# The sending tables of the last five node blocks are made first, the receiving tables behind everything, in a graph-network kernel

## The chip, the cores and the metric

The kernel runs on one core of a Trainium2 chip. The core has five engines with an instruction queue each: TensorE (PE, with its weight loads counted apart as PEld), VectorE (DVE), ScalarE (ACT), GpSimd (POOL) and SyncE (SP). SyncE and ScalarE issue ordinary transfers, GpSimd issues gathers; all are carried by the core's 16 DMA engines. The metric is the device time of the program in microseconds (us); lower is better.

## What is computed

A graph has N = 3125 nodes with 128 features, and 100000 edges, sorted by their destination. Each edge has 16 attributes and one of R = 4 types. Two layers follow each other; shortened:

```python
# layer 0
summed = segment_sum(x[src], dst)
x = layernorm(x + elu(summed / max(deg, 1) @ W + b))
# layer 1, with h = x, four heads of 128 columns, HC = 512
xl = einsum('nf,rfh->nrh', h, W_l) + b_l
xr = einsum('nf,rfh->nrh', h, W_r) + b_r
z = leaky_relu(xl[src, edge_type] + xr[dst, edge_type] + e_feat, 0.2)
score = einsum('ehc,ehc->eh', z, att[edge_type])
alpha = softmax of score over the edges with one dst and one edge_type
agg = segment_sum(xl[src, edge_type] * alpha, dst * R + edge_type)
h1 = layernorm(h + gate-weighted mean over types and heads of agg)
x = layernorm(x + layernorm(h1 + ffn(h1)))
```

`xl` is called the sending table here: row (node, type) is what a node gives to its outgoing edges. `xr` is the receiving table: what a node adds to its incoming edges.

## The kernel before

**Tiling.** Edges are cut into 784 tiles of 128; four tiles are a unit u, so there are 196 units. Nodes are cut into 25 blocks of 128 (`NB2` = 25). Edges are sorted by destination, so a tile receives at a few neighbouring nodes, but its sources lie anywhere.

**Layer 0, up to about 1080 us.** For each tile GpSimd gathers x[src] (64 KB), TensorE sums the rows by destination and VectorE adds the result to `acc0`. When the edges of a block are through, `block(b, s)` (line 1263) finishes the block in small steps: `take`, `mean` and `stats` (normalization), `turn` (transpose to `ht`), `tables` and `half`. They are put into a table of steps with `at_step`, and the loop over s (lines 1362 to 1402) issues each step's pieces on the engines in an order written out by hand; blocks 20 to 24 have steps pressed closer together. The class `Ordered` (line 629) fixes this order on each engine, and since it issues the instructions, most of them carry its line, 647, in the profile.

**Tables.** For each type r, `tables` has TensorE make a receiving tile `xq` and a sending tile `xp`, 128x512 each, in PSUM: one matmul with the bias (`two`, `cbl`), then h times `wr` or `wl`. Three PSUM buffers `xp` serve both. ScalarE copies the sending tile and four more columns to `xlr` (line 647, three buffers). `half(r)`, one step later, has SyncE write `xlr` to the DRAM table `xl_d` (258 KB), VectorE split the receiving tile into a rounded high part and the remainder (`xh`, three buffers; a copy and a subtraction), and SyncE write both parts to the DRAM table `xr_d` (512 KB). There are 100 of each over the run. Each block also writes its `ht` to `ht_d`.

**Between the layers.** ScalarE's queue loads all of `ht_d` into `acc1` (1600 KB). Constants are made, and flags are computed that say whether the edges suit this tiling (`bad`, 15 columns, lines 1476 to 1534); if not, the function `general` runs afterwards. Three of the ten buffers `xl` serve these flags as scratch.

**Attention, to about 2750 us.** The loop over s (from -2) does parts of several units per step. SyncE loads the codes of a unit (`sg`, `lb`, `load_codes`), its attributes `ers` and masks `rm`, and the windows `win` of the receiving table (`load_rows`, 15 buffers, lines 1561 to 1578). GpSimd gathers four tiles of `xl_d` per unit, 258 KB each, into `xl` (`load`, ten buffers, so up to ten units ahead, of which three wait for the flags' scratch). `z_of` sums one head's edge features, the window picked by a one-hot (`oht`) and the transposed `xl` on TensorE into `z`; ScalarE makes `relu`, TensorE the `row` of scores, VectorE the softmax, and TensorE the weighted sums `ag`, which VectorE adds to `acc1`. The only order across engines is that of data and of buffers. Buffers of all these lie in one pool, `at` (line 1408), whose memory layer 0 used before; DRAM tables are tracked as a whole, so a read of `xr_d` or `xl_d` waits for every write to it that was issued before.

**After attention.** The feed-forward part and two normalizations, some 60 us.

Of the kernel before, what the change touches and what calls it, by code (L numbers as in the profile page):

```python
# [20 lines left out]
P = 128  # L21
N = 3125
E = 100000
F = 128
R = 4
H = 4
HC = H * F
# [17 lines left out]
F32R = mybir.dt.float32r  # L45
# [573 lines left out]
WW = 16  # L619
# [9 lines left out]
NP = 3200  # L629
NB2 = NP // P  # L630
NPW = NP + WQ
XW = HC + H
RW = 4 * P + 2
# [30 lines left out]


UD, ND, SHI = 72, 240, NB2
SEG = ((0, 52), (52, UD))


# [23 lines left out]
def windows(ctx: ExitStack, tc: tile.TileContext, a, out, flag):  # L693
    nc = tc.nc
    cst = ctx.enter_context(tc.tile_pool(name="cst", bufs=1))
    dram = ctx.enter_context(tc.tile_pool(name="fdram", bufs=1, space=DRAM))
# [6 lines left out]
    lb_d = dram.tile([NQ // 4, P, 16 * H * R], F32, name="lb_d")  # L703
    v2_d = dram.tile([P, H], F32, name="v2_d")
    xl_d = dram.tile([NP * R, XW], F32, name="xl_d")
    xr_d = dram.tile([NP * R * 2, HC], F32, name="xr_d")
    h_d = dram.tile([NB2, P, F], F32, name="fh_d")
    ht_d = dram.tile([P, NP], F32, name="ht_d")
    ident = cst.tile([P, P], F32, name="f_ident")
# [4 lines left out]
    tb = S["tb"] = cst.tile([16, 2 * TT + 1], BF16, name="tb")  # L714
    tk = S["tk"] = cst.tile([16, 2 * TT], BF16, name="tk")
    ns2 = S["ns2"] = cst.tile([16, 2 * TT], BF16, name="ns2")
    bad = cst.tile([P, 15], F32, name="bad")
    iw = cst.tile([P, P], F32, name="iw")
    pid = cst.tile([P, 1], I32, name="pid")
    ir = cst.tile([P, R], F32, name="ir")  # L720
# [12 lines left out]
    def of_tile(t, col):  # L733
        return bass.IndirectOffsetOnAxis(ap=col[:, t:t + 1], axis=0)

    xr_n = xr_d.rearrange("(n k) c -> n k c", k=2 * R)

    def node(t, eng):
        return nc.values_load(d0_i[0:1, t:t + 1], engines=[eng], min_val=0, max_val=N - 1,
# [17 lines left out]
    with tc.tile_pool(name="l0c", bufs=1) as l0c:  # L757
# [14 lines left out]
        with tc.tile_pool(name="pr", bufs=1) as pr, tc.tile_pool(name="prp", bufs=2, space=PSUM) as prp:  # L772
# [94 lines left out]
            rm = pr.tile([TR, TC, RW], BF16, name="rm")  # L867
            b, k, f, l = (rm[:, :, o:o + P] for o in (0, P + 2, 2 * P + 2, 3 * P + 2))
# [14 lines left out]

        with tc.tile_pool(name="m0c", bufs=1) as m0c, tc.tile_pool(name="l0", bufs=2) as l0, \
                tc.tile_pool(name="l0e", bufs=1) as l0e, tc.tile_pool(name="m0", bufs=2) as m0, \
                tc.tile_pool(name="l0p", bufs=1, space=PSUM) as l0p, \
                tc.tile_pool(name="m0p", bufs=1, space=PSUM) as m0p:
            pe, ve, act, sp = (Ordered(tc, e) for e in (nc.tensor, nc.vector, nc.scalar, nc.sync))
# [15 lines left out]
            wr = m0c.tile([F, R, HC], F32, name="wr")  # L904
            fb = wl.rearrange("p r w -> p (r w)")[:, :TT]

            cbl = m0c.tile([P, R, XW], F32R, name="cbl")
            two = m0c.tile([P, 2, P], F32R, name="two")
# [73 lines left out]
            def halves(s, r, p0, row, n):  # L982

                d = {}

                def high():
                    d["hi"] = m0.tile([1, 2, XW], F32R, name="xh", bufs=3)
# [270 lines left out]


            xl_v = xl_d.rearrange("(b p r) w -> b p r w", p=P, r=R)  # L1260
            xr_v = xr_d.rearrange("(b p r s) w -> b p r (s w)", p=P, r=R, s=2)

            def block(b, s):
                n = min(P, N - b * P)
                d = {}

                def new(name, shape, bufs=3, dt=F32):
                    d[name] = m0.tile(shape, dt, name=name, bufs=bufs)
                    return d[name]
# [37 lines left out]
                def turn():  # L1307
                    sp.dma_start(h_d[b], d["y0"])
                    htp = m0p.tile([P, F], F32, name="mw")
                    pe.transpose(htp, d["y0"], ident)  # L1310
                    act.activation(new("ht", [P, F], 2), htp, AF.Copy)

                def tables():
                    xa = m0p.tile([P, R, H], F32, name="mw")
                    pe.matmul(xa, two[:, 0], cbl[:, :, HC:], start=True, stop=False)
                    pe.matmul(xa, d["ht"], wl[:, :, HC:], start=False, stop=True)
                    for r in range(R):
                        xp, xq = (m0p.tile([P, HC], F32, name="xp", bufs=3) for _ in range(2))
                        for o, w, i, c in ((xq, wr[:, r], 1, cbl[:, r, :HC]), (xp, wl[:, r, :HC], 0, cbl[:, r, :HC])):
                            pe.matmul(o, two[:, i], c, start=True, stop=False)  # L1320
                            pe.matmul(o, d["ht"], w, start=False, stop=True)
                        xl = d["xl", r] = m0.tile([P, XW], F32, name="xlr", bufs=3)
                        xh = d["xh", r] = m0.tile([P, 2, HC], F32R, name="xh", bufs=3)
                        act.activation(xl[:, :HC], xp, AF.Copy)
                        act.activation(xl[:, HC:], xa[:, r], AF.Copy)
                        d["xq", r] = xq

                def half(r):
                    if r == 0:
                        sp.dma_start(ht_d[:, b * P:(b + 1) * P], d["ht"])  # L1330
                    xh = d["xh", r]
                    sp.dma_start(xl_v[b][:, r], d["xl", r])
                    ve.tensor_copy(xh[:, 0], d["xq", r])
                    ve.tensor_sub(xh[:, 1], d["xq", r], xh[:, 0].bitcast(F32))
                    sp.dma_start(xr_v[b][:, r], xh.bitcast(F32).rearrange("p s w -> p (s w)"))

                if b >= NB2 - 5:
                    at_step(s - 2, "sp", early)
# [21 lines left out]
            for s in range(last + 1):  # L1360
# [40 lines left out]
                for us in edges:  # L1401
                    keep(us)


    acc1 = ctx.enter_context(tc.tile_pool(name="ac1", bufs=1)).tile([P, NPW], F32, name="acc1")
    nc.gpsimd.memset(acc1[:, NP:], 0.0)
    nc.scalar.dma_start(acc1[:, :NP], ht_d)
    with tc.tile_pool(name="ac", bufs=1) as ac, tc.tile_pool(name="at", bufs=2) as at, \
            tc.tile_pool(name="atp", bufs=1, space=PSUM) as atp:


# [60 lines left out]
        nc.vector.tensor_scalar(acc1[:, :NP], acc1[:, :NP], gbt, None, op0=OP.add)  # L1472


        rf, rl, rs = (at.tile([P, 4, XW], F32, name="xl", bufs=10).rearrange("p a b -> p (a b)") for _ in range(3))
        nc.sync.dma_start(rf[:16, :2 * TT], bass.AP(tensor=fl_d.tensor, offset=fl_d.offset, ap=[[0, 16], [1, 2 * TT]]))
        rF, rL = (rf[:16, i * TT:(i + 1) * TT] for i in range(2))
        rF4, rL4 = (x[0:1].rearrange("p (u i) -> p u i", i=4) for x in (rF, rL))
# [48 lines left out]
        count(7, NQ)  # L1527
        o1 = ac.tile([P, 1], F32, name="o1")
        nc.vector.memset(o1, 1.0)
        bp = atp.tile([1, 15], F32, name="row", bufs=2)  # L1530
# [20 lines left out]

        def load_codes(u):
            d = Q[u] = {}
            d["sg"] = at.tile([P, 512], BF16, name="sg", bufs=4)
            sv = S["seg_d"][u * 4:u * 4 + 4, :]
            sp.dma_start(d["sg"], bass.AP(tensor=sv.tensor, offset=sv.offset, ap=[[0, P], [1, 512]]))
            if u % 4 == 0:
                LB[u // 4] = at.tile([P, 4, 4, H, R], F32, name="lb")
                sp.dma_start(LB[u // 4].rearrange("p j t h r -> p (j t h r)"), lb_d[u // 4])

        def load_rows(u):
            d = Q[u]
            d["er"] = ers[:, u % NE]
            sp.dma_start(d["er"][:2 * DE].bitcast(F32), eat_d[u])
            if u % 2 == 0:
                g = G[u // 2] = {}
                g["rm"] = at.tile([P, RW], BF16, name="rm", bufs=6)
                rv_ = S["rm_d"][u * 4:u * 4 + 8, :]
                sp.dma_start(g["rm"], bass.AP(tensor=rv_.tensor, offset=rv_.offset, ap=[[RW, 8], [0, 16], [1, RW]]))

            d["w"] = []
            for i, k in windows_of(u):
                n = WW if k > 1 else W
                n4 = node(u * 4 + i, ENG.SP)
                w = at.tile([P, HC], F32R, name="win", bufs=15)
                sp.dma_start(w[:n * 2 * R].bitcast(F32), xr_n[ds(n4, n)].rearrange("n k c -> (n k) c"))
                d["w"].append((w, slice(i * P, (i + k) * P), n * 2 * R))

        def load(u):
            d = Q[u]  # L1580
            d["xl"] = at.tile([P, 4, XW], F32, name="xl", bufs=10)
# [402 lines left out]
```

## Time and profile before

| what | value |
|---|---|
| three runs | 2867.88, 2873.77, 2883.67 us |
| median | 2873.77 us |
| profiled execution, as a run | 2875.92 us |
| its span, first to last instruction | 2874.1 us |
| mean granted TensorE clock | 0.898 |
| PE busy | 2417.7 us (84%) |
| DVE busy | 1821.4 us (63%) |
| POOL busy | 1245.1 us (43%) |
| ACT busy | 908.9 us (32%) |
| gathers of `xl_d` | 784, 959 ns each on POOL |
| VectorE's copy to `xh`, 128x512 | 100, 690 ns each |
| ScalarE's copy to `xlr`, 128x512 | 100, 597 ns each |

How to read it: a profile line begins with a time or a line and engine, then an operation with what it writes and reads. "Idle before" is the gap before an instruction on its own engine, with what ended it; "issue" is a gap in which the engine waited for nothing that the profile shows. The rows of digits cut the span into 40 slices of 71.9 us and give the busy tenths of each. The chain of waits goes back from the last instruction, at each step to what released it. A table by stretches gives, for each stretch of time, the busy time of each engine with the number of its instructions, the granted clock, the share of the DMA engines that was busy, and GB/s.

### The profile page before, as it was taken

What the parts mean: (1) busy time and instruction counts of PE and PEld (TensorE: products, weight loads), DVE (VectorE), ACT (ScalarE), POOL (GpSimd) and SP (SyncE); (2) the same over time, 40 slices, a digit from 0 to 9 for tenths busy, and PEclk for the clock granted to TensorE, in tenths of its full rate; (3) what the DMA queues carried; (4) which work ended last, traced back from release to release, by engine and by line L of the source; (5) the groups of instructions that cost most, each with busy time, mean ns of one, the idle gap of its engine ahead of it and who ended that gap; (6) DMA issues with size and microseconds to landing.
All of it is one profiled execution on the core that took longest, in us unless ns stands there. A gap on an engine that the chain in (4) does not pass through costs nothing.

```text
span 2874.1 us, 66163 instructions
## 1 busy us (share of the span) xinstructions
PE 2417.7 (84%) x24485; PEld 1858.4 (65%) x24485; DVE 1821.4 (63%) x6395; ACT 908.9 (32%) x1964; POOL 1245.1 (43%) x1294
## 2 busy tenths in 40 slices
PE   3687777877777685699999999999999999999974
PEld 2454454445444443577777777888888888888853
DVE  6655535653544345377777777777777777776656
ACT  0121112212222231244444444444444443333314
POOL 6555443444434413244444444444444444444400
PEclk9757778878888787799999999999999999999977
DMA  4323344444455456466666667777777789999910
GB/s 128 90 73 104 112 137 142 138 125 155 147 186 173 139 197 227 128 210 205 205 205 208 205 205 216 235 236 235 236 235 233 235 241 245 254 243 246 236 53 24
DMA packets 284394, 520.64 MB, mean 181 GB/s; under 512 B 45833, under 2 KB 144820, under 8 KB 283151
## 3 DMA queue, kind: packets, MB, share of 16 engines
q1 hardware_dynamic: 201588, 273.76, 30.7%
q0 software_dynamic: 78592, 239.71, 29.6%
q8 instruction: 194, 3.18, 0.5%
q10 hardware_dynamic: 3880, 2.84, 0.4%
q14 instruction: 140, 1.15, 0.1%
HBM read 412.10 MB, written 104.82 MB: 180 GB/s over the span
## 4 chain that ended last, share of the span: by engine, by line
PE 48%; DVE 8%; issue 3%; DMA 2%; ACT 0%; SPq 0%; DVEq 0%; ACTq 0%
PE z L647 30%; PE ag L647 7%; PE row L647 6%; DVE wo L647 4%; PE e L647 2%; PE sm_p L647 2%; DMA win<-xr_d 1%; DVE f L647 0%; DVE oh L647 0%; DVE ea L647 0%; PE f L1930 0%; PE f L1922 0%; DVE acc L647 0%; DMA xr_d<-xh 0%; DVE fst L1886 0%
## 5 line engine op out<-in xcount | busy, mean ns | idle before, releaser
L647 POOL DMA_INDIRECT xl<-xl_d,src_e x784 | 751.5, 959 | 895.8 <-PE ag L647 391.5
L647 POOL DMA_INDIRECT xg<-in_x_dram,src_e x496 | 489.0, 986 | 542.6 <-PE sg L647 368.5
L647 ACT ACTIVATE relu<-z 128x512 f32<-128x512 f32 x784 | 449.1, 597 | 793.7 <-PE z L647 611.1
L647 PE MATMUL z<-f_ident,xl 128*128 128x128 f32 x3136 | 476.1, 274 | 0.0
L647 PEld LDWEIGHTS z<-f_ident,xl 128*128 128x128 f32 x3136 | 368.7, 141 | 44.3 <-issue 0.6
L647 PE MATMUL z<-ea,weh 128*128 128x512 f32 x784 | 360.9, 460 | 18.4 <-issue 14.1
L647 PE MATMUL z<-oht,win 96*128 96x128 f32 (+2 forms) x1600 | 343.4, 297 | 4.1 <-DMA win<-xr_d 2.2
L647 PEld LDWEIGHTS z<-oht,win 128*128 128x128 f32 (+1 forms) x1600 | 275.4, 190 | 60.6 <-issue 3.2
L647 PE MATMUL z<-ea,wel 128*128 128x512 f32 x784 | 310.1, 395 | 0.1
L647 PE MATMUL row<-relu,attw 128*32 128x128 f32 x6272 | 247.7, 277 | 31.1 <-issue 29.4
L647 PE MATMUL ag<-xl,wo 128*32 128x128 f32 x6272 | 225.6, 279 | 7.5 <-DVE acc L647 4.2
L647 PEld LDWEIGHTS row<-relu,attw 128*32 128x32 f32 x6272 | 172.6, 109 | 85.0 <-issue 84.0
L647 PE MATMUL xp<-cbl,two 128*128 128x512 f32 x200 | 165.4, 827 | 30.5 <-DVE xh L647 13.1
L647 DVE TENSOR_TENSOR acc<-acc,fo 128x128 f32 x124 | 35.3, 285 | 245.0 <-remote 97.9
L647 PEld LDWEIGHTS ag<-xl,wo 128*32 128x32 f32 x6272 | 181.1, 112 | 9.1 <-DVE acc L647 5.1
L647 DVE TENSOR_TENSOR_SCAN m<-rm,row 128x128 f32<-128x128 bf16 x98 | 41.2, 420 | 228.4 <-PE row L647 228.4
L647 PE MATMUL fo<-ic,il 128*128 128x300 bf16 x744 | 153.5, 357 | 37.4 <-DVE acc L647 31.3
L647 DVE CAST xh<-xp 128x512 fp32r<-128x512 f32 x100 | 69.0, 690 | 157.3 <-PE xp L647 113.7
L647 PEld LDWEIGHTS z<-ea,weh 128*128 128x128 f32 x784 | 149.5, 191 | 27.5 <-issue 27.5
L647 ACT ACTIVATE xlr<-xp 128x512 f32<-128x512 f32 x100 | 59.7, 597 | 304.3 <-PE xp L647 156.2
L647 PEld LDWEIGHTS z<-ea,wel 128*128 128x128 f32 x784 | 150.1, 191 | 9.0 <-issue 0.4
L647 DVE SCALAR_TENSOR_TENSOR ea<-far,e 128x512 fp32r<-128x512 bf16 x196 | 132.2, 675 | 36.7 <-remote 35.6
(327 smaller groups left out, 4059.3 us busy)
## 6 DMA issues: line engine op xcount, KB each, us to landing
win<-xr_d SPq DMA_DIRECT2D x224, 256.0 KB
xr_d<-xh SPq DMA_DIRECT2D x100, 512.0 KB
win<-xr_d SPq DMA_DIRECT2D x176, 192.0 KB
xl_d<-xlr SPq DMA_DIRECT2D x100, 258.0 KB
sg<-seg_d SPq DMA_DIRECT2D x196, 128.0 KB
rm<-rq_d SPq DMA_DIRECT2D x98, 128.5 KB
eat_d<-emt SPq DMA_DIRECT2D x196, 64.0 KB
xl<-xl_d,src_e POOLq DMA_INDIRECT x784
```

Of the source, the lines that this page charges most:

```text
L647: ins = f(*args, **kw)
```

## The change

The last five blocks (`NL` = 5, blocks 20 to 24) make only their sending tables in `tables`. Their receiving tables follow after the whole loop over steps, in a loop of their own over 20 (block, type) pairs; there ScalarE, not VectorE, makes the high part, and ScalarE's queue, not SyncE's, issues the write. The transposed blocks `ht` are kept for this in five buffers.

The receiving table becomes two DRAM tables. Blocks 0 to 19 go to `xr_a`; blocks 19 to 24 go to `xr_b`, so block 19 is written to both. Units below `UL` = 175 take their windows from `xr_a`, the others from `xr_b`. Two more flags check that the edges allow this.

What the receiving tables need (`wr`, `cbl`, `two`, `xh`, `ht`) moves to a pool `m0r` of its own. Attention's buffers are split into three pools: `ax` for `xl`, `ay` for `sg`, `lb`, `rm` and `win`, `at` for the rest; numbers of buffers stay.

```diff
+NL, UL = 5, 175
-    xr_d = dram.tile([NP * R * 2, HC], F32, name="xr_d")
+    xr_a, xr_b = (dram.tile([NP * R * 2, HC], F32, name=n) for n in ("xr_a", "xr_b"))
-    bad = cst.tile([P, 15], F32, name="bad")
+    bad = cst.tile([P, 17], F32, name="bad")
+                tc.tile_pool(name="m0r", bufs=1) as m0r, \
...
+            def table(o, ht, w, i, r):
+                pe.matmul(o, two[:, i], cbl[:, r, :HC], start=True, stop=False)
+                pe.matmul(o, ht, w, start=False, stop=True)
+
+            def receiving(b, r, xq, copy):
+                xh = m0r.tile([P, 2, HC], F32R, name="xh", bufs=3)
+                copy(xh[:, 0], xq)
+                ve.tensor_sub(xh[:, 1], xq, xh[:, 0].bitcast(F32))
+                return [(x[b][:, r], xh.bitcast(F32).rearrange("p s w -> p (s w)"))
+                        for x, y in ((xra_v, b < NB2 - NL), (xrb_v, b >= NB2 - NL - 1)) if y]
...
-                    act.activation(new("ht", [P, F], 2), htp, AF.Copy)
+                    d["ht"] = HT[b] = m0r.tile([P, F], F32, name="ht", bufs=NL)
+                    act.activation(d["ht"], htp, AF.Copy)
...
                     for r in range(R):
-                        xp, xq = (m0p.tile([P, HC], F32, name="xp", bufs=3) for _ in range(2))
-                        for o, w, i, c in ((xq, wr[:, r], 1, cbl[:, r, :HC]), (xp, wl[:, r, :HC], 0, cbl[:, r, :HC])):
-                            pe.matmul(o, two[:, i], c, start=True, stop=False)
-                            pe.matmul(o, d["ht"], w, start=False, stop=True)
+                        if b < NB2 - NL:
+                            xq = d["xq", r] = m0p.tile([P, HC], F32, name="xp", bufs=3)
+                            table(xq, HT[b], wr[:, r], 1, r)
+                        xp = m0p.tile([P, HC], F32, name="xp", bufs=3)
+                        table(xp, HT[b], wl[:, r, :HC], 0, r)
...
                     sp.dma_start(xl_v[b][:, r], d["xl", r])
-                    ve.tensor_copy(xh[:, 0], d["xq", r])
-                    ve.tensor_sub(xh[:, 1], d["xq", r], xh[:, 0].bitcast(F32))
-                    sp.dma_start(xr_v[b][:, r], xh.bitcast(F32).rearrange("p s w -> p (s w)"))
+                    if b < NB2 - NL:
+                        for o, x in receiving(b, r, d["xq", r], ve.tensor_copy):
+                            sp.dma_start(o, x)
...
+            for b in range(NB2 - NL, NB2):
+                for r in range(R):
+                    xq = m0p.tile([P, HC], F32, name="xp", bufs=3)
+                    table(xq, HT[b], wr[:, r], 1, r)
+                    for o, x in receiving(b, r, xq, lambda o, x: act.activation(o, x, AF.Copy)):
+                        act.dma_start(o, x)
...
-    with tc.tile_pool(name="ac", bufs=1) as ac, tc.tile_pool(name="at", bufs=2) as at, \
+    with tc.tile_pool(name="ac", bufs=1) as ac, tc.tile_pool(name="ax", bufs=10) as ax, \
+            tc.tile_pool(name="ay", bufs=2) as ay, tc.tile_pool(name="at", bufs=2) as at, \
             tc.tile_pool(name="atp", bufs=1, space=PSUM) as atp:
...
+        nc.vector.tensor_scalar(bad[0:1, 15:16], rL[0:1, 4 * UL - 1:4 * UL], float(P * (NB2 - NL) - WW), None,
+                                op0=OP.is_gt)
+        nc.vector.tensor_scalar(bad[0:1, 16:17], rF[0:1, 4 * UL:4 * UL + 1], float(P * (NB2 - NL - 1)), None,
+                                op0=OP.is_lt)
...
-                sp.dma_start(w[:n * 2 * R].bitcast(F32), xr_n[ds(n4, n)].rearrange("n k c -> (n k) c"))
+                sp.dma_start(w[:n * 2 * R].bitcast(F32),
+                             (xra_n if u < UL else xrb_n)[ds(n4, n)].rearrange("n k c -> (n k) c"))
```

More of the change, by code (lines that the diff above doesn't have):

```diff
@@ L734, in of_tile @@
         return bass.IndirectOffsetOnAxis(ap=col[:, t:t + 1], axis=0)
-    xr_n = xr_d.rearrange("(n k) c -> n k c", k=2 * R)
+    xra_n, xrb_n = (x.rearrange("(n k) c -> n k c", k=2 * R) for x in (xr_a, xr_b))
     def node(t, eng):
@@ L903, in windows @@
             wl = m0c.tile([F, R, XW], F32, name="wl")
-            wr = m0c.tile([F, R, HC], F32, name="wr")
+            wr = m0r.tile([F, R, HC], F32, name="wr")
             fb = wl.rearrange("p r w -> p (r w)")[:, :TT]
-            cbl = m0c.tile([P, R, XW], F32R, name="cbl")
-            two = m0c.tile([P, 2, P], F32R, name="two")
+            cbl = m0r.tile([P, R, XW], F32R, name="cbl")
+            two = m0r.tile([P, 2, P], F32R, name="two")
             nc.vector.memset(cbl.bitcast(F32), 0.0)
@@ L986, in high @@
                 def high():
-                    d["hi"] = m0.tile([1, 2, XW], F32R, name="xh", bufs=3)
+                    d["hi"] = m0r.tile([1, 2, XW], F32R, name="xh", bufs=3)
                     act.activation(d["hi"][:, 0, :n], row()[:, :n], AF.Copy)
@@ L1260, in windows @@
             xl_v = xl_d.rearrange("(b p r) w -> b p r w", p=P, r=R)
-            xr_v = xr_d.rearrange("(b p r s) w -> b p r (s w)", p=P, r=R, s=2)
+            xra_v, xrb_v = (x.rearrange("(b p r s) w -> b p r (s w)", p=P, r=R, s=2) for x in (xr_a, xr_b))
+            HT = {}
+            def table(o, ht, w, i, r):
[7 more added lines that the diff above has]
+                        for x, y in ((xra_v, b < NB2 - NL), (xrb_v, b >= NB2 - NL - 1)) if y]
             def block(b, s):
@@ L1317, in tables @@
                     for r in range(R):
-                        xp, xq = (m0p.tile([P, HC], F32, name="xp", bufs=3) for _ in range(2))
-                        for o, w, i, c in ((xq, wr[:, r], 1, cbl[:, r, :HC]), (xp, wl[:, r, :HC], 0, cbl[:, r, :HC])):
-                            pe.matmul(o, two[:, i], c, start=True, stop=False)
-                            pe.matmul(o, d["ht"], w, start=False, stop=True)
+                        if b < NB2 - NL:
[3 more added lines that the diff above has]
+                        table(xp, HT[b], wl[:, r, :HC], 0, r)
                         xl = d["xl", r] = m0.tile([P, XW], F32, name="xlr", bufs=3)
-                        xh = d["xh", r] = m0.tile([P, 2, HC], F32R, name="xh", bufs=3)
                         act.activation(xl[:, :HC], xp, AF.Copy)
                         act.activation(xl[:, HC:], xa[:, r], AF.Copy)
-                        d["xq", r] = xq
                 def half(r):
@@ L1330, in half @@
                         sp.dma_start(ht_d[:, b * P:(b + 1) * P], d["ht"])
-                    xh = d["xh", r]
                     sp.dma_start(xl_v[b][:, r], d["xl", r])
-                    ve.tensor_copy(xh[:, 0], d["xq", r])
-                    ve.tensor_sub(xh[:, 1], d["xq", r], xh[:, 0].bitcast(F32))
-                    sp.dma_start(xr_v[b][:, r], xh.bitcast(F32).rearrange("p s w -> p (s w)"))
+                    if b < NB2 - NL:
+                        for o, x in receiving(b, r, d["xq", r], ve.tensor_copy):
+                            sp.dma_start(o, x)
                 if b >= NB2 - 5:
@@ L1472, in windows @@
         nc.vector.tensor_scalar(acc1[:, :NP], acc1[:, :NP], gbt, None, op0=OP.add)
-        rf, rl, rs = (at.tile([P, 4, XW], F32, name="xl", bufs=10).rearrange("p a b -> p (a b)") for _ in range(3))
+        rf, rl, rs = (ax.tile([P, 4, XW], F32, name="xl", bufs=10).rearrange("p a b -> p (a b)") for _ in range(3))
         nc.sync.dma_start(rf[:16, :2 * TT], bass.AP(tensor=fl_d.tensor, offset=fl_d.offset, ap=[[0, 16], [1, 2 * TT]]))
@@ L1529, in windows @@
         nc.vector.memset(o1, 1.0)
-        bp = atp.tile([1, 15], F32, name="row", bufs=2)
+        bp = atp.tile([1, 17], F32, name="row", bufs=2)
         nc.tensor.matmul(bp, o1, bad, start=True, stop=True)
@@ L1553, in load_codes @@
             d = Q[u] = {}
-            d["sg"] = at.tile([P, 512], BF16, name="sg", bufs=4)
+            d["sg"] = ay.tile([P, 512], BF16, name="sg", bufs=4)
             sv = S["seg_d"][u * 4:u * 4 + 4, :]
@@ L1557, in load_codes @@
             if u % 4 == 0:
-                LB[u // 4] = at.tile([P, 4, 4, H, R], F32, name="lb")
+                LB[u // 4] = ay.tile([P, 4, 4, H, R], F32, name="lb")
                 sp.dma_start(LB[u // 4].rearrange("p j t h r -> p (j t h r)"), lb_d[u // 4])
@@ L1566, in load_rows @@
                 g = G[u // 2] = {}
-                g["rm"] = at.tile([P, RW], BF16, name="rm", bufs=6)
+                g["rm"] = ay.tile([P, RW], BF16, name="rm", bufs=6)
                 rv_ = S["rm_d"][u * 4:u * 4 + 8, :]
@@ L1574, in load_rows @@
                 n4 = node(u * 4 + i, ENG.SP)
-                w = at.tile([P, HC], F32R, name="win", bufs=15)
-                sp.dma_start(w[:n * 2 * R].bitcast(F32), xr_n[ds(n4, n)].rearrange("n k c -> (n k) c"))
+                w = ay.tile([P, HC], F32R, name="win", bufs=15)
+                sp.dma_start(w[:n * 2 * R].bitcast(F32),
+                             (xra_n if u < UL else xrb_n)[ds(n4, n)].rearrange("n k c -> (n k) c"))
                 d["w"].append((w, slice(i * P, (i + k) * P), n * 2 * R))
@@ L1580, in load @@
             d = Q[u]
-            d["xl"] = at.tile([P, 4, XW], F32, name="xl", bufs=10)
+            d["xl"] = ax.tile([P, 4, XW], F32, name="xl", bufs=10)
             for i in range(4):
```

## The prediction

> **What bounds the kernel now.** I read the page first: which engine fills which stretch of the span, and which chain ended last.
>
> ```profile
> span 2874.1 us, 66163 instructions
> PE   3687777877777685699999999999999999999974
> DMA  4323344444455456466666667777777789999910
> PE 48%; DVE 8%; issue 3%; DMA 2%; ACT 0%; SPq 0%; DVEq 0%; ACTq 0%
> ```
>
> From about 1190 us on (slice 17 of 40) TensorE is at nine tenths or more: attention is TensorE's, and no line of the change alters what TensorE does there. Before that nothing is full. So the change can only move the moment at which attention reaches its full speed, and every microsecond of that is a microsecond of the whole. Next I took the chain of waits around that moment:
>
> ```profile
> 1104.18 7.41 PE xp L647 x21
> 1111.58 1.52 issue
> 1113.10 0.67 ACT xlr L647 x2
> 1113.79 0.32 SPq L647
> 1114.20 8.05 DMA xr_d<-xh
> 1122.45 0.32 SPq L1476
> ...
> 1128.73 4.08 DMA ers<-eat_d
> 1132.81 0.25 issue
> 1133.06 4.64 PE z L647 x14
> ...
> 1172.92 0.37 PE row L647
> 1173.29 2.42 issue
> ```
>
> The last block's tables end at 1113, the last receiving write lands at 1122.25, and then everything that attention loads is let go at once. The first z (a 128x512 score tile) starts at 1133.06. But TensorE then falls into single instructions with 1 to 2.5 us of "issue" between them. The table by stretches and GpSimd's timeline tell when:
>
> ```profile
> 1115.00:1120.00 5.00, 0.00 (x0) 0.00 (x0) 1.89 (x1) 0.00 (x0) 0.00 (x0) 0.74 0.99 395
> 1130.00:1140.00 10.00, 6.89 (x27) 5.38 (x28) 8.75 (x27) 2.51 (x4) 7.56 (x9) 0.61 1.03 329
> 1160.00:1170.00 10.00, 1.53 (x4) 0.51 (x4) 0.00 (x0) 0.00 (x0) 7.56 (x9) 0.50 0.76 209
> 1180.00:1190.00 10.00, 10.00 (x81) 8.17 (x81) 4.01 (x11) 4.36 (x9) 0.00 (x0) 0.89 0.21 68
> 1123.21 0.95 POOL L647 DMA_INDIRECT xl<-xl_d,src_e  x1 [39.67 <-DVE xl L1493]
> 1173.55 0.95 POOL L647 DMA_INDIRECT xl<-xl_d,src_e  x1 [0.30 <-issue]
> ```
>
> (Columns of the stretches: length, busy PE, weight load, DVE, ACT, POOL, granted clock, DMA share, GB/s.) Forty gathers of the sending table go out back to back, one per 1.254 us, from 1123.21 to 1173.55; from the 16th on PE, DVE and ACT hardly move, and all is full again near 1178, 3.5 us after the last. I call this the stutter. It isn't bytes: the same shows at the start of layer 0, where gathers run unbroken from 50.67 to 76.7 at a DMA share of 0.18 to 0.21 and PE, ACT and DVE stand still until 80. In attention proper, four gathers per 7.9 us do no harm. By 1143 TensorE had done some 9 us of attention, so the kernel before is worth an attention that starts at full speed at 1177.8 - 9 = about **1168.5**. That is my zero.
>
> **What the Trainium skill says.** "Runtime: NRT & Kernel Launch", Instruction fetch mechanics: each engine has a small first-in-first-out memory of instructions, refilled in 16 KiB blocks over a DMA queue of its own. That fits the stutter: the trace has two packets on the q8 instruction queue between 1100 and 1185, at 1102.4 and 1182.1, and none in the stutter. That a stream of gathers keeps the refill out no run here shows; I use it as a guess. "DMA: Bandwidth & Descriptors", Issuing engines are not separate DMA queues: writes from ScalarE's queue run on the same 16 engines as SyncE's and GpSimd's. The trace agrees: 1130 to 1140 has gathers and loads together at a share of 1.03 and 329 GB/s. So moving the receiving writes to ScalarE saves issue time only, not transfer time.
>
> **The change part by part.** All against the profiled execution (span 2874.1 us, 2875.9 us as a run; the median of the three runs is 2873.8, so I subtract from that).
>
> *Send side, sooner.* A table costs TensorE 1.09 us (1069.49, 1070.58, 1071.67 in its timeline). Blocks 20, 21, 22 lose four receiving tables each, 12 x 1.09 = 13 us. After the last layer-0 gather (1033.8) nothing comes from outside, and each burst of eight tables (8.8 us; block 22's runs to 1073.8) stands in TensorE's order ahead of the aggregation that the next block waits for, so I take the whole 13 as path: layer 0's last additions from 1077 to 1064. Blocks 23 and 24 lose 8 x 1.09 = 8.7 us out of 1091.05 to 1113.0. Tables end near 1113 - 13 - 8.7 = 1091; ScalarE's copy and its four columns 0.8, SyncE's issue 0.3, landing of 258 KB on a queue that is no longer full about 2.5 us instead of 8.05: the last sending write lands near 1095, the first gather starts near **1096** instead of 1123.2, and GpSimd's stream ends near 1096 + 50 = 1146. Bounds: 20 us (half of the 13 hidden) to 32 us sooner. The gathers no longer wait for any receiving write.
>
> *Receive side, later.* All 20 tables of blocks 20 to 24 stand in TensorE's order ahead of attention's first e and z, and attention's general pool lies on the memory of xh, so VectorE's first memset of a carry, the one-hots queued behind it and TensorE's first z wait for the landing of the last xr_b write. The start of attention is therefore T = last xr_b landing + 1.5 us. Per table: TensorE 1.09, ScalarE's copy 0.60 (as the 128x512 xlr copy), VectorE's subtraction 0.69, ScalarE's issue about 0.4, a 512 KB write. By engine time alone that is 1.1 us each. But xh has three buffers and a copy waits for the write three before it: with a landing of 2.5 us (empty queue) a round of three takes 0.6 + 0.7 + 0.4 + 2.5 = 4.2, 1.4 us a table; with the 8 us that a full queue showed, 9.7 / 3 = 3.2 us a table. Besides, about 15 us of VectorE's flag work and the 1.89 us addition on acc stand between the first six subtractions.
>
> *Bytes.* From 1092 on: 20 x 0.524 = 10.5 MB of writes, 40 gathers = 10.6 MB, acc 1.6 MB, and the first windows, codes and rows, about 3.5 MB (counted from the issues between 1100 and 1185): 26 MB. GpSimd's pitch holds gathers to 210 GB/s; 330 to 395 GB/s in all leaves 120 to 185 for the writes, which is 10.5 MB in 57 to 87 us while gathers run, faster once they end. Half a gather stream at 175 GB/s carries 9.5 MB by 1146, the rest goes at twice that: the last write lands near 1154, and T = **1155 to 1157**. Nothing of TensorE's first units waits then, since all 40 gathers have landed and no stream is left to stutter.
>
> *Small edits.* Block 19's four extra 0.512 MB writes fall where the DMA share is about a half: nothing, at most 4 x 1.4 = 5.6 us if SyncE's queue were full. VectorE loses 20 casts (13.8 us), part of the path already counted; ScalarE takes 20 x 0.6. Two more flag checks, 0.3 us under other work. The selection of xr_a or xr_b is made when the program is built; unit 175 comes near 2600 us, long after the writes. Windows of units below 175 read xr_a, whole by then. The three pools only decide who waits for whose memory, counted above; the same 10 and 15 buffers remain, so attention's pace stays.
>
> *Sum.* 1156 - 1168.5 = -12.5 us: 2873.8 - 12.5 = **2861**.
>
> **The rivals.**
>
> *The receive side is quick.* If transfers are shared in favour of the writes (4 KB rows beside the gathers' 2 KB) and flags cost nothing, tables pass at 1.5 to 2 us: 1092 + 20 x 2 = 1132 to 1145, T = 1133 to 1147, time 2838 to 2852. For it: 395 GB/s in 1115 to 1120. Against it: TensorE's last block already had landings of 8 us with no gathers beside them.
>
> *The stutter falls on the receive side (the slower end).* It begins about 20 us into the stream, 1116, and lasts until 1150. In it TensorE passed one load and matmul per 2.5 us; a table has three, so 34 us pass 4 or 5 tables. Then T = 1150 + 2 x (tables left) + 1.5, with 2 us a table. With 6 done by 1116 (the flags stand there) about 10 are left: T = 1172, +3 us; with 3 done, and 3 us for each of 13 left, T = 1190, 2895. It decides from about 8 tables left (1167.5, no gain); beyond 15 left the kernel is slower beyond doubt. For it: ACT and DVE stood still too. Against it: the receive side has only some 120 PE instructions, and TensorE did about 150 matmuls and weight loads between the packet of 1102.4 and its first faltering at 1143.
>
> *The change doesn't bring the gathers forward.* If the bursts of blocks 20 to 22 lay beside VectorE's chain, gathers start near 1105 and T moves to 1160 to 1168: 2865 to 2873. A failing boundary check would run the general path instead, at far more; the squared-uniform destinations put unit 175 near node 2510, inside its limits of 2432 and 2544.
>
> **How the numbers follow.** Forecast case (T 1148 to 1163, 2853 to 2869): 0.42. Quick: 0.16. Stutter on the receive side (2869 to 2896): 0.34. Not forward: 0.08. A difference under 0.5%, 14.4 us, can't be told from none here. Faster (below 2859.4): all of the quick case and half of the forecast case, 0.37. Slower (above 2888.2): the later part of the stutter case and what I may have missed of waits on shared memory, 0.26. The same: 0.37. The range leaves out the quickest of the quick and the worst of the stutter: 2842 to 2892; the forecast case's own is 2853 to 2869.
>
> **What would show it.** The first xl gather near 1096 (right) or past 1105 (send side misjudged). Twenty xh copies on ScalarE, with waits for xr_b landings of 6 to 9 us (bytes decide) or with "issue" (stutter). The first z 1.5 us behind the last xr_b landing, near 1156, and then TensorE full without single instructions. I am wrong if TensorE stutters after the first z, if the first z comes past 1170, or if stretches from 1300 on hold TensorE less busy than before (48.04 of 50 us in 1900 to 1950).

## The result, and the profile after

| | before | after |
|---|---|---|
| median of 20 runs each | 2869.58 us | 2862.89 us |
| lowest, highest | 2854.74, 2888.87 | 2845.42, 2878.52 |
| ratio, 95% interval | | 0.9977 [0.9955, 0.9998] |
| profiled execution: run, span | 2875.92, 2874.1 us | 2866.84, 2865.0 us |

The change is worth 6.7 us, 0.23%, with an interval of 0.6 to 12.9 us: less than half a per cent. As a difference, 12.5 us were forecast. The median lies 2 us from the forecast of 2861, and that is in part luck: the kernel before has a median of 2869.6 in 20 runs, 4.2 us below the 2873.8 of the three runs from which the forecast subtracts.

The chain of waits of the kernel after, in the stretch that answers to the one shown of before (start, length, what ran or was waited for):

```profile
1087.61 4.46 PE xp L647 x12
1092.09 6.64 DMA xl<-fl_d
1098.76 0.96 DVE xl L1506
1099.72 0.89 DVE xl L1507
1100.60 0.60 DVE xh L647
...
1117.44 8.47 DMA xr_b<-xh
1126.04 1.31 issue
1127.35 6.78 DMA xr_b<-xh
...
1149.23 5.91 another core or an unknown queue
1155.16 0.60 ACT xh L647
...
1163.62 2.63 DMA xr_b<-xh
1166.36 0.73 ACT far L647
1167.11 0.70 DVE ea L647
1167.85 4.62 PE z L647 x14
```

Sending tables end at 1092, the first z starts at 1167.85, 1.6 us behind the landing of the last receiving write, and from there TensorE runs without a hole. The stretches of the kernel after (length, busy PE, PEld, DVE, ACT, POOL, granted clock, DMA share, GB/s), and its first and last early gather from GpSimd's timeline:

```profile
1110.00:1120.00 10.00, 7.60 (x10) 2.50 (x9) 6.75 (x16) 1.79 (x3) 7.56 (x9) 0.50 1.03 402
1130.00:1140.00 10.00, 6.43 (x12) 2.61 (x12) 2.08 (x3) 1.88 (x4) 7.56 (x9) 0.84 1.02 413
1150.00:1160.00 10.00, 3.85 (x5) 0.83 (x3) 1.38 (x2) 1.19 (x2) 2.69 (x3) 0.50 0.68 267
1170.00:1180.00 10.00, 10.00 (x80) 8.20 (x79) 2.13 (x5) 4.21 (x8) 0.00 (x0) 0.88 0.24 73
1100.90 2.22 POOL L647 DMA_INDIRECT xl<-xl_d,src_e  x1 [28.48 <-DVE xl L1507]
1152.36 0.95 POOL L647 DMA_INDIRECT xl<-xl_d,src_e  x1 [0.30 <-issue]
```

The gathers now lie beside the receiving tables, at a DMA share of 1.02 to 1.03. A whole run hides 6.7 us in a spread of 30, so I compare milestones, counted from the last gather of layer 0. "Unit 10" is the moment at which ScalarE starts that unit's `far`, an early step of a unit; by then each kernel runs at attention's own pace.

| us | last sending write issued | to first xl gather | to first z | to unit 10 | sum |
|---|---|---|---|---|---|
| before | 80.9 | 9.4 | 9.9 | 96.5 | 196.7 |
| after | 56.9 | 7.9 | 67.0 | 59.6 | 191.4 |

The send side is 25.5 us sooner, the stutter after the first z is gone (37 us), and 57 us of receiving tables stand before the first z. The balance is 5.3 us. The two profiles differ by 9.1: layer 0 ended 3.2 us later in the kernel after, the milestones give 5.3 us back, and 7.0 us lie behind unit 10, where the second pair below shows 1.1.

### The profile page after: what moved, and what is told of

It is laid out like the page before. It is cut to its first block, busy times and chain, and to the rows that moved or that the text cites. A ratio compares the mean times of both kernels' runs of the same rounds, so it can differ in the third digit from the quotient of the medians.

```text
span 2865.0 us, 66148 instructions
## 1 busy us (share of the span) xinstructions
PE 2418.8 (84%) x24485; PEld 1853.0 (65%) x24485; DVE 1809.5 (63%) x6377; ACT 920.2 (32%) x1984; POOL 1242.4 (43%) x1294
## 4 chain that ended last, share of the span: by engine, by line
PE 51%; DVE 9%; issue 3%; DMA 2%; another core or an unknown queue 1%; ACT 1%; DVEq 0%; ACTq 0%; SPq 0%
PE z L647 30%; PE ag L647 7%; PE row L647 6%; DVE wo L647 4%; PE e L647 2%; PE xp L647 2%; PE sm_p L647 2%; PE fo L647 1%; DMA xr_b<-xh 1%; PE mw L647 1%; DMA win<-xr_b 0%; DVE oh L647 0%; DVE f L647 0%; DVE xh L647 0%
## 5 line engine op out<-in xcount | busy, mean ns | idle before, releaser
L647 PE MATMUL row<-relu,attw 128*32 128x128 f32 x6272 | 239.0, 276 | 5.4 <-issue 3.8
L647 PE MATMUL fo<-ohq,sgs 128*128 128x64 f32 x496 | 93.2, 322 | 83.6 <-issue 55.5
L647 PEld LDWEIGHTS fo<-ohq,sgs 128*128 128x128 f32 x496 | 87.0, 243 | 105.4 <-issue 63.8
L647 ACT ACTIVATE xlr<-xp 128x512 f32<-128x512 f32 x100 | 59.7, 597 | 284.1 <-PE xp L647 143.0
```

The source lines that it names most:

```text
L647: ins = f(*args, **kw)
```

## Experiments

**A first set: what is the stutter, and what holds the receive phase?** Four kernels. Theory S blames the long unbroken stream of gathers, theory B counts bytes and buffers alone. In the expectations, what is called unit 5's codes is unit 10's `far` (a slip in the name; the times are unit 10's). The holding edit, in the kernel after and, with pool `at`, in the kernel before:

```diff
+        def held(u):
+            d = Q.setdefault(u, {})
+            d["xl"] = ax.tile([P, 4, XW], F32, name="xl", bufs=10)
+            ve.memset(d["xl"][:, 0, 0:1], 0.0)
...
             part(masked, s, 0, 1, NQ)
+            if 4 <= s + 2 < 10:
+                held(s + 2)
```

> The changed kernel, but the gathers of units 4 to 9 are held back: each waits for a one-element memset of its buffer that VectorE does two units of attention earlier, so at most 16 gathers go out in one piece before the first z, and the other 24 follow at attention's pace. Theory S (a long unbroken stream of gathers keeps the other engines from their instructions): the holes of 1144 to 1158 in the receive phase vanish, which is 9 us, and 6.4 MB less lie in the way of the receiving writes, which is 6.4 MB at 410 GB/s or 15 us; first z near 1143 instead of 1167.9, no stutter after it, and the whole about 20 to 25 us below the changed kernel. Theory B (only bytes and buffers count): first z near 1152, then TensorE is short of gathers, and the whole gains 5 us at most.

> The same holding of the gathers of units 4 to 9 in the kernel before the change. Theory S: first z near 1133 as before, but no single-instruction stretch from 1143 to 1178; unit 5 comes some 33 us sooner, and the whole is near 2836, a ratio of 0.988, which would also be below the changed kernel. Theory B: the same bytes have to come after the same writes, so the time moves by no more than 5 us.

The third replaces the early gathers by plain loads:

```diff
+            if s == 0:
+                for v in range(7):
...
+                    for i in range(4):
+                        k = (v * 4 + i) * P
+                        sp.dma_start(d["xl"][:, i], xl_d[k:k + P, :])
```

> The changed kernel, but the sending rows of units 0 to 6 are not gathered: SyncE loads as many rows of the same table, in one piece, into the same buffers (7 units, 28 loads of 258 KB), so the values of these units are not the reference's, the bytes are the same, and GpSimd issues only the 12 gathers of units 7 to 9. Theory S: no stream, no holes: the last ten tables pass at 2.7 us or less, last xr_b landing near 1157, first z near 1158 instead of 1167.9. Theory B: bytes are what they were, first z within 3 us of 1167.9.

The fourth moves the addition on acc1 into attention, and was meant to move the load of acc1 behind the receiving writes as well:

```diff
-    nc.scalar.dma_start(acc1[:, :NP], ht_d)
...
+        act.dma_start(acc1[:, :NP], ht_d)
...
+            if s == 4:
+                ve.tensor_scalar(acc1[:, :NP], acc1[:, :NP], gbt, None, op0=OP.add)
```

> The changed kernel, but the 1600 KB load of acc1 stands on ScalarE's queue behind the twenty receiving writes, and its addition of the bias four units into attention. My reading of the late first gather (1100.9, where 1096 was forecast): the last xl_d write shared its transfer time with this load. Then the last xl_d write lands in 3 us instead of 7, the first gather starts near 1096, and the first z comes 3 to 5 us sooner, near 1164. Rival: the gathers wait for the flags' work on VectorE, which waits for its own load; then the first gather stays near 1100.

These ran on another chip, where the kernel before took 2550.25 us: layer 0's last gather starts at 785 to 797 there instead of 1033. Ratios to the kernel before: after with held gathers 1.0101 [1.0056, 1.0147], before with held gathers 1.0006 [0.9983, 1.0028]. Single runs: plain loads 2582.72 us, late acc1 2585.87 us. The expectations compare the variants with the kernel after on the first chip, and that kernel didn't run on this one; here all three are slower than the kernel before. So the first question became what the two kernels do on this chip.

The fourth kernel isn't what its text says. By its trace ScalarE's queue issues the load of acc1 at 847.34, 2.9 us before the last sending write (850.25); in the kernel after it is 1090.10 against 1093.02, the same distance. Only the addition moved, to 941.5. So this run can't tell whether the load delays the first gather.

**A second set: both kernels again, and the split alone.**

> The kernel before, unchanged, for its profile on this chip: the runs with held gathers came from a chip that grants more clock in layer 0 (whole kernel before: 2550 us), and the profiles compared so far are from two chips. If theory S holds everywhere, the profile has the stretch of single instructions from the 16th gather on, some 35 us, and unit 5's codes come 105 us after the first gather as on the first chip (1123.2 to 1229.6); if the stutter belongs to the first chip or is a matter of where a refill falls, unit 5 comes about 70 us after the first gather, as with held gathers.

> The changed kernel, unchanged, for time and profile on this chip. By the sums on the first chip (receive phase 1093 to 1166) the first z comes 75 us after the last sending table and 67 us after the first gather. Theory B: on any chip the receive phase lasts 65 to 75 us, since its bytes are the same, so against a kernel before that doesn't stutter the change loses 25 to 30 us (ratio 1.01), and against one that does it gains 2 to 10.

```diff
+    xr_a, xr_b = (dram.tile([NP * R * 2, HC], F32, name=n) for n in ("xr_a", "xr_b"))
...
-                    sp.dma_start(xr_v[b][:, r], xh.bitcast(F32).rearrange("p s w -> p (s w)"))
+                    for x, y in ((xra_v, b < NB2 - NL), (xrb_v, b >= NB2 - NL - 1)):
+                        if y:
+                            sp.dma_start(x[b][:, r], xh.bitcast(F32).rearrange("p s w -> p (s w)"))
```

> The kernel before with one part of the change alone: the receiving table in two DRAM tables, block 19 written to both, units from 175 on reading the second; order and buffers as before. On the first chip the changed kernel gained 5 us of its 9 between unit 174 and the end (187.0 us from unit 174's to unit 195's codes before, 181.7 after). If that comes of the second table, this run has 182 us there; if it is run to run, it has anything from 180 to 188, and the kernel before run again differs from 187 as well.

This chip was of the first kind: before 2897.66 us, after 2888.70, ratio 0.9966 [0.9945, 0.9987]. The stutter repeats, with unit 10 at 109 us after the first gather, and so do the milestones: before 81.3 + 9.6 + 9.8 + 99.1 = 199.8, after 57.2 + 8.8 + 67.0 + 59.3 = 192.3; the gain to unit 10 is 7.5 us. The split alone has 199.2, one profile against one: the two DRAM tables bring nothing by themselves that this can show. From unit 10 to unit 174 the two kernels of each pair agree within 0.1 us (1322.1 and 1322.0, 1334.1 and 1334.1). From unit 174 to unit 195 it takes 181.4 us, the kernel before run again 179.7 and the kernel after again 179.7, against the first pair's 187.0 and 181.7: that part was run to run.

**A third set: held gathers again.**

> The kernel before, unchanged, as the partner of the next two on their chip. On a chip that takes about 2870 to 2900 us, theory S expects the stutter (unit 5's codes 105 to 109 us after the first gather, as 106.4 and 108.9 before). On a chip that takes about 2550 us, unit 5 comes about 70 us after the first gather and no stretch of single instructions is in it; then held gathers have nothing to remove there, which is why they changed nothing (ratio 1.0006) in the first set.

> The kernel before with the gathers of units 4 to 9 held back. Theory S: on a chip with the stutter, unit 5's codes come about 70 us after the first gather instead of 105 to 109, and the whole falls by about 36 us (ratio 0.987), below the changed kernel too; on a chip without it, ratio 1.000 again. Theory B: ratio 1.000 on either.

> The changed kernel with the gathers of units 4 to 9 held back. On a chip with the stutter, theory S: first z about 50 us after the first gather instead of 67, as in the first set (865.8 to 917.2), no stutter after it, and the whole some 15 to 20 us below the changed kernel, though above the held kernel before, whose first z comes 10 us after the first gather. Theory B: first z within 5 us of 67 after the first gather.

The chip of this set was of the second kind (before 2548.95 us). The profile of the unchanged kernel before there, by stretches:

```profile
870.00:880.00 10.00, 0.00 (x0) 0.00 (x0) 4.60 (x31) 0.61 (x1) 3.13 (x4) 0.51 0.69 242
880.00:890.00 10.00, 4.98 (x15) 3.59 (x16) 9.73 (x26) 1.43 (x3) 7.87 (x8) 0.50 1.03 298
890.00:900.00 10.00, 9.95 (x83) 7.87 (x83) 3.77 (x12) 4.50 (x8) 7.59 (x8) 0.97 1.05 342
900.00:910.00 10.00, 10.00 (x114) 8.17 (x113) 6.22 (x19) 5.00 (x10) 7.72 (x8) 1.00 1.00 321
910.00:920.00 10.00, 10.00 (x96) 8.18 (x97) 4.96 (x15) 5.46 (x11) 7.68 (x8) 1.00 0.93 303
```

GpSimd's gathers go out at nearly the same pitch from 875.96 to 926.72, at a DMA share of 0.93 to 1.05, and TensorE is full from 890 on. The same program, the same stream of 40 gathers, and no stutter. Held gathers therefore had nothing to remove: 1.0006 [0.9979, 1.0034]. Nor did the holding break the stream much in the kernel before; with TensorE at full pace gaps of 2 to 3 us appeared only from the 21st gather on, four to eight gathers apart. The kernel after with held gathers took 2567.87 us in a single run.

**A fourth set: the kernel after on a chip without the stutter.**

> The kernel before with the gathers of units 4 to 9 held back, a third time, since neither chip so far on which it ran has the stutter (before: 2550 and 2549 us there, and the profile of the kernel before shows TensorE full at 890, 14 us after its first gather). On a chip that takes 2870 to 2900 us for the kernel before: if the unbroken stream is the cause of the stutter there, unit 5's codes come about 70 us after the first gather instead of 106 to 109, ratio 0.987, and it is faster than the changed kernel; if something else in the transition causes it, unit 5 stays at 100 or more and the ratio at 1.00. On a chip of 2550 us: 1.000 again.

> The changed kernel, unchanged, on the same chip. On a chip of 2870 to 2900 us: ratio 0.996 to 0.998 as on two such chips. On a chip of 2550 us, where the kernel before loses nothing after its first z, the first z comes some 65 us after the first gather against 10 before, with the first gather 15 us sooner, so the change costs 25 to 35 us: ratio 1.010 to 1.014, slower. If the change gained there as well, my zero, the equivalent start of the kernel before, would be wrong.

Again the second kind (before 2552.09 us). Held gathers before: 1.0015 [0.9987, 1.0043]. The kernel after: 2580.75 us, ratio **1.0113 [1.0072, 1.0153]**: the change costs 29 us there, as expected. Milestones:

| us, second kind | last sending write issued | to first xl gather | to first z | to unit 10 | sum |
|---|---|---|---|---|---|
| before | 76.1 | 9.6 | 9.8 | 59.8 | 155.3 |
| after | 57.3 | 8.0 | 62.8 | 59.7 | 187.8 |

Send side and receive phase differ by 5 us at most from the first kind. Only the step from the first z to unit 10 differs by much, 59.8 against 96.5 us, and only in the kernel before. That is nearly the whole difference between a small gain and a clear loss. The receive phase without any stutter, from the chain of waits of the kernel after on this chip:

```profile
844.65 6.81 DMA xl<-fl_d
...
877.44 6.60 DMA xr_b<-xh
884.12 0.61 ACT xh L647
884.75 0.70 DVE xh L647
885.48 6.69 DMA xr_b<-xh
892.25 0.61 ACT xh L647
892.88 0.70 DVE xh L647
893.61 6.82 DMA xr_b<-xh
```

A round is 8.1 us (877.44, 885.48, 893.61): a landing of 6.7, ScalarE's copy, VectorE's subtraction. Three buffers of xh, so three tables a round, 2.7 us each.

What the other variants say of this phase, measured from the last sending write to the first z on chips of the second kind: after 70.8; held gathers 60.0 and 58.9; plain loads 74.5; late acc1, whose load didn't move, 70.5. Plain loads with the same bytes don't shorten it, so on this kind of chip it isn't GpSimd's stream as such that holds it. With held gathers 16 instead of 40 gathers go out before the first z, 6.3 MB less, and the phase is 11 to 12 us shorter; the first z comes 51 us after the first gather in both, where theory B of the first set had put it (1152, against the first chip's 1100.9). That speaks for bytes, in one profile each.

The last sending write takes some 7 us to land instead of the 2.5 of the forecast, and the DMA packets in the trace of the kernel after tell where the time goes. The load of acc1 moves its packets from 1091 to 1097.5. Between 1092 and 1095 it has the DMA engines to itself, at a share of 0.90, and SyncE's queue, with the last sending writes and the flags' load in it, moves none; the last packet of the sending writes ends at 1099.6. That the load of acc1 holds them up is read from this order and not shown: no run has the load later.

With held gathers the writes free themselves at the end. ScalarE's timeline of that kernel, in the first set:

```profile
897.27 0.60 ACT L647 ACTIVATE xh<-xp 128x512 fp32r<-128x512 f32 x1 [1.20 <-DMA xr_b<-xh]
898.62 0.34 ACTq L647 DMA_DIRECT2D xr_b<-xh  x1
899.07 0.60 ACT L647 ACTIVATE xh<-xp 128x512 fp32r<-128x512 f32 x1 [1.20 <-DVE xh L647]
900.42 0.34 ACTq L647 DMA_DIRECT2D xr_b<-xh  x1
900.86 0.60 ACT L647 ACTIVATE xh<-xp 128x512 fp32r<-128x512 f32 x1 [1.20 <-DVE xh L647]
```

A table takes 1.80 us here with the DMA engines a third idle: ScalarE's issue of a write waits for VectorE's subtraction, and the next copy stands behind that issue. So 20 tables in this order can't take less than 36 us on this queue, whatever the transfers do.

**Not tried:** held gathers on a chip of the first kind, so that whether breaking up the stream removes the stutter there stays open; and the kernel after with the load of acc1 really moved. On the chips of the second kind no variant was faster than the kernel before; on the first kind the split is the only one, and its single run of 2909.43 us isn't faster either.

## Why the prediction came out as it did

**Right: where the time would be won and paid.** On the chips of the first kind it was the moment of attention's full speed that moved, by the milestones; attention's own pace stayed, as from unit 10 to unit 174. The zero was put at 1168.5: from the first z to unit 10 an undisturbed attention takes 59.6 us, and the kernel before reaches unit 10 at 1229.6, so its equivalent start was 1170.0. The other repeat (before again) has 99.1 in place of 96.5, so the loss in the stutter is 37 to 40 us.

**Right in the sum: the send side.** First gather forecast 27 us sooner, measured 25.5 from the last layer-0 gather and 22.3 by the clock, since layer 0 itself ended 3.2 us later in that execution. Layer 0's last additions come 14 us sooner after that gather, where 13 were forecast: the tables that were left out did lie on the path. Up to the issue of the last sending write the gain is 24.0 us (about 22 forecast), behind it 1.5 us (5.5 forecast, since the landing was put at 2.5 us). That the two errors nearly cancel is luck.

**Mis-sized: T.** Forecast 1156, which is 60 us after the first gather of 1096; measured 67.0 after the first gather. Two terms of the sum were short. First, the bytes were counted from 1092, 4 us before the first gather, with the flags named but not charged. ScalarE's timeline of the kernel after shows what happened:

```profile
1093.19 0.60 ACT L647 ACTIVATE xh<-xp 128x512 fp32r<-128x512 f32 x1 [0.38 <-PE xp L647]
1101.24 0.35 ACTq L647 DMA_DIRECT2D xr_b<-xh  x1
1101.64 0.60 ACT L647 ACTIVATE xh<-xp 128x512 fp32r<-128x512 f32 x1 [7.85 <-DVE xh L647]
...
1142.59 0.60 ACT L647 ACTIVATE xh<-xp 128x512 fp32r<-128x512 f32 x1 [2.08 <-issue]
1143.94 0.34 ACTq L647 DMA_DIRECT2D xr_b<-xh  x1
1147.48 0.60 ACT L647 ACTIVATE xh<-xp 128x512 fp32r<-128x512 f32 x1 [4.29 <-issue]
1148.83 0.34 ACTq L647 DMA_DIRECT2D xr_b<-xh  x1
1155.16 0.60 ACT L647 ACTIVATE xh<-xp 128x512 fp32r<-128x512 f32 x1 [7.09 <-remote]
1156.51 0.34 ACTq L647 DMA_DIRECT2D xr_b<-xh  x1
```

The first copy is done at 1093.79, but its subtraction stands in VectorE's order behind two flag operations that wait for their load, which is issued at 1092.09 and lands in 6.64 us; the first write goes out at 1101.24, 0.3 us after the first gather. So the start comes 4.3 us later than in the forecast, both counted from that gather. From 1117 to 1144 a write goes out every 2.7 us, at 402 to 415 GB/s, somewhat better than the 3.0 us that 175 GB/s make. Second, a hole: between 1143.94 and 1160.04 three writes take 16.1 us where 8.1 were due. The chip without it has 62.8 instead of 67.0 from first gather to first z, so it costs 4.2 us net. 4.3 us at the start and 4.2 in the hole, less 1.5 that the quicker pace gave back, are the 7.0.

The first term needs no mechanism that the forecast didn't name. The hole does. ScalarE's copy of 1155.16 needs the buffer of the write issued at 1141.26, three writes before it. By the DMA packets that write was through at 1147.18, 8.0 us before the copy; the next one was through at 1149.72, 9.0 us before its copy (1158.69). For the seven writes before them this step takes 0.7 to 0.8 us but for the last (3.1), and in the kernel after on the second kind it stays at 0.7 to 0.8 to the end. The repeat on the first kind has 9.0 and 9.3. So the hole is neither slow transfers nor slow matrix work (TensorE's tables of 1148.85 and 1156.54 pass without gaps): late in the stream it is the news of a landing that comes late. Why, no run shows.

**The rivals.** The quick receive side fell: at 413 GB/s the DMA engines were full. ScalarE's queue alone, at 1.8 us a table from 1101, would have allowed a T near 1140, inside that rival's range. The stutter on the receive side came true in a small way: it began 43 us into the stream, not 20, with five writes left, not ten tables, and as late news of landings, not as single instructions of TensorE. On its slower end it was wrong about this chip, but the slower outcome is real for another reason: on a chip where attention doesn't stutter, nothing pays for the receive phase. The forecast took the stutter as a property of the program. That it depends on the chip could not be read from one execution, and its own price (37 us of cover) was in the text without the question what happens if it goes.

**The guess on its cause fell.** The refill of instructions isn't late, as far as counts show. In the kernel before, the packets on the q8 queue at 1102.4 and 1182.1 have 125 weight loads and 116 matmuls between them; in the kernel before on a chip without stutter, the packets at 900.3 and 913.4 have 133 and 131. The next block came when about as many instructions were used up, so TensorE doesn't seem to have lacked them. How slowly it took them, from TensorE's matmul and weight-load timelines of the kernel before:

```profile
1164.51 0.37 PE L647 MATMUL row<-relu,attw 128*32 128x128 f32 x1 [2.38 <-issue]
1167.31 0.37 PE L647 MATMUL row<-relu,attw 128*32 128x128 f32 x1 [2.43 <-issue]
1165.92 0.13 PEld L647 LDWEIGHTS row<-relu,attw 128*32 128x32 f32 x1 [2.68 <-issue]
1168.71 0.12 PEld L647 LDWEIGHTS row<-relu,attw 128*32 128x32 f32 x1 [2.66 <-issue]
```

Load, matmul, load, matmul: 1164.51, 1165.92, 1167.31, 1168.71, one instruction every 1.40 us while the gathers run. That the gathers do it is supported by where it begins and ends, in three executions on two chips, and not shown: the same stream does nothing on a chip of the second kind.

One rival stands untested. For the same 2898 to 2902 transfers issued, the traces of the first kind hold 20891 to 21753 of the updates by which transfers tell that they have landed, those of the second kind 42349 to 42516. From 25 to 50 us after the first gather the kernel before has 42 and 37 of them on the first kind, with 20 transfers issued, and 569 on the second, with 35. So the first kind has about half as many of these records, and fewest of all in the stutter. A gap marked "issue" can there be a wait whose update isn't in the trace, and the recording itself may be what slows the engines and the news of landings. Every time on record has a recorded span and clock beside it, so no run here separates the chip from the recording of it.

**Readings a little off.** Three of the prediction's readings are slightly wrong and decide nothing. Forty gathers from 1123.21 to 1173.55 are 1.29 us apart on average (1.25 between most), 205 GB/s and not 210; a weight load and matmul took 2.8 us in the stutter, not 2.5; and the row of digits is at nine from slice 18 on, not 17.

## What to carry to other kernels

A change that moves work under a stall is worth what the stall was worth on that chip; ask what the change costs where the stall is absent, and profile both kernels on more than one chip before keeping it. Here the same change is 0.9977 and 0.9966 on two chips and 1.0113 on a third. Compare executions by milestones inside the span (last gather, first z, tenth unit), since a spread of 30 us hides 7, and a late part that differs in one pair may agree in the next. Look in the trace whether an edit moved what it was meant to move, before its result is read: the load of acc1 stayed where it was. And price a chain through an engine's queue by everything that stands in it: a DMA issue that waits for another engine holds the copy behind it.

## What the runs showed of the hardware

Two kinds of chips: the kernel before takes 2870 to 2898 us on two of them and 2549 to 2552 us on three, with mean granted clocks of 0.898 to 0.901 and 0.93 to 0.94 (kernel before in layer 0: 0.80 and 0.89; in attention 1.00 on both). Three quarters of the 322 us between two profiles of the kernel before lie in layer 0, whose last gather starts at 1033 to 1059 and at 782 to 802; 37 us are the stutter, 34 us attention between units 10 and 174. What causes the difference no run here shows. The traces of the first kind hold about half as many landing records as those of the second.

On the first kind a stream of 40 gathers, most of them 1.25 us apart, goes with one TensorE instruction per 1.40 us; on the other kind the same stream, at a DMA share of 0.93 to 1.05, leaves TensorE full in the one profile of it. In the kernel after, a copy started 8.0 to 9.3 us after the last packet of the write that it waited for late in the stream on the first kind, and 0.7 to 0.8 us on the second. Gathers and 512 KB writes together moved 402 to 416 GB/s over stretches of 10 us on both kinds.
